# Setup of a cross-attention and expert kernel: TensorE multiplies by nought until the context is there, loads in order of need, query weights transposed between the keys' products

## The chip, the core and the metric

The kernel runs on one core of a Trainium2 chip. The metric is device time in microseconds (us). The engines of the core are TensorE (PE in the profile; PEld is its weight load), VectorE (DVE), ScalarE (ACT), GpSimd (POOL) and SyncE (SP), which here only issues transfers. Each engine works through its own instructions in order and waits on semaphores for the others; transfers (DMA) run in queues beside them. PSUM is the memory TensorE writes to, eight banks of which this kernel uses in turn; SBUF is the memory for everything else.

## The reference

Four sequences of 1024 tokens of width 256 attend to a context of 77 rows each, and then pass through a mixture of nine experts, two per token.

```
x = x + xattn(latents=layernorm(x), context=ctx)     # 16 heads of 64
    xn = layernorm(context) * ln1_w + ln1_b ;  ln = layernorm(latents) * ln2_w + ln2_b
    q = (ln @ Wq) * (1 + fside) + fside ;  k, v = split(xn @ Wkv)
    out = softmax(q k^T / 8) v @ Wout
x = x + moe(layernorm(x))                             # router, top 2 of 9, silu(x Wg) * (x Wu) @ Wd
```

All is float32. Since the context is short, the kernel folds Wq and the keys into one matrix per sequence (`g`, 256 by 16 x 77), and the values and Wout into another (`u`), so that a token needs only its normalised row times `g`, a softmax, and the weights times `u`. Building `g` and `u` is the setup; it is where the change lies.

## The kernel before, in words

The instructions of each engine stand in the order of the source (`tc.manual_schedule()`); the framework adds the semaphores. Four stages follow each other: the setup of `g` and then of `u` (to about 62 us), attention over 32 groups of 128 tokens with the routing of the group before mixed in, and the experts. TensorE passes from one to the next.

The setup up to `g`, with the lines of the profile:

- Constants. `make_identity` on GpSimd; on VectorE `eps_t`, 18 small memsets for `rank` and `base` (L109, L110), `ones`, `seen`.
- Loads. ScalarE issues `wrow` (ln2_w repeated on all partitions, L346) and `fs` (fside on all partitions, L350). SP issues the context `cx` in two transfers (L375), `wq_sb` in four, `wk_sb` in four (L380), then `wv_sb`, `wo_sb` and the first two groups of `x`. GpSimd issues ln1_w and ln1_b as columns `cw`, `cb` (L357), then `qb`, the router's weights, and a fill of a list in DRAM (L396).
- Context. Four BNStats and four aggregations on VectorE (L402, L404), a root on ScalarE (L408), and the normalised rows `cn`: sequences 0 and 2 on ScalarE (L444), 1 and 3 on VectorE (L439). TensorE transposes them into two banks `pct` (L452). ScalarE (L461) and VectorE (L456) each bring one of the two halves to SBUF as `cT`, times `cw` plus `cb`.
- Query weights. TensorE transposes `wq_sb` in 16 pieces into four banks `pwq` (L417), ahead of the context's transposes. VectorE multiplies them by `wrow` into `wqT` (L427): the first quarter before `cT`, the others between the keys' products. `wlast` (L498) is the last column negated, which ScalarE adds to each row (L503).
- Offsets. VectorE copies `fs` into `shift` by two copies (L471), makes `scale1` (L473) and scales `shift` (L474), and clears `cfold` (L476). In before they stand behind its half of `cT`. `scale1` is read by `kTs`.
- Keys. For each of eight pairs of heads TensorE makes `pk` from `wk_sb` and both halves of `cT` (L485), ScalarE copies it to `kT` (L489), VectorE scales it into `kTs` (L490).
- `g`. TensorE multiplies `wqT` by `kTs` (L626), and VectorE and ScalarE take the results out of PSUM in turn (L144, L146). In between stand the query offset `pcq`, the router's weights and a few tables.

A row of the trace such as `x32` for `pk` counts two records for each float32 matmul. On GpSimd, four memsets that the later stage needs follow the list's fill: `vbd`, `vrem` and two for `u` (L565 to L574). The first is held by hand until VectorE's last `cn` is done:

```
first = nc.gpsimd.memset(vbd, 0.0)
tc.add_manual_dep(first.ins, normed.ins.name, ...)
```

Of the kernel before, what the change touches and what calls it, by code (L numbers as in the profile page):

```python
# [8 lines left out]
F32 = mybir.dt.float32  # L9
I32 = mybir.dt.int32  # L10
U32 = mybir.dt.uint32
AF = mybir.ActivationFunctionType
ALU = mybir.AluOpType
AX = mybir.AxisListType

P = 128
# [5 lines left out]
def kernel(  # L22
# [18 lines left out]
    nc = tc.nc  # L41

    B, N, D = x.shape
    J = ctx_in.shape[1]
# [3 lines left out]
    E, _, FF = wg.shape  # L48
    C = D // P
    NP = H // 2  # L50
    TOK = B * N
    TB = 512
    NS = TB // P
# [41 lines left out]
    const = ctx.enter_context(tc.tile_pool(name="const", bufs=1))  # L95
# [5 lines left out]
    ident = const.tile([P, P], F32, name="ident")  # L101
    make_identity(nc, ident)
    eps_t = const.tile([P, 1], F32, name="eps_t")
    nc.vector.memset(eps_t, EPS)

    rank = const.tile([P, NS, E], F32, name="rank")
    base = const.tile([P, NS, E], F32, name="base")
    for e in range(E):
        nc.vector.memset(rank[:, :, e : e + 1], float(E - e))  # L109
        nc.vector.memset(base[:, :, e : e + 1], float(e * TOK))  # L110
    ones = const.tile([P, P], F32, name="ones")
    nc.vector.memset(ones, 1.0)
    seen = const.tile([P, E], F32, name="seen")
# [14 lines left out]
    def mm_tile(name):  # L128
        return ps_mm.tile([P, TB], F32, tag="mm", name=name)
# [3 lines left out]
    def bank_tile(name):  # L133

        turn_of[0] = (turn_of[0] + 1) % 8
        if turn_of[0] < 5:
            return mm_tile(name)
        k = turn_of[0] - 5
        return ps_sc.tile([P, TB], F32, tag=f"sc{k}", name=name)
# [10 lines left out]
    g_half, u_half = {}, {}  # L150
# [3 lines left out]
        u_half[i] = apool.tile([P, BH, KC, DE], F32, name=f"u{i}")  # L154
    g_sb = [g_half[b // BH][:, b % BH] for b in range(B)]
    u_sb = [u_half[b // BH][:, b % BH] for b in range(B)]

    def moments(src, n, name):
        k = src.shape[1]
        st = stat.tile([P, k, 6], F32, tag="bn", name=f"bn_{name}")  # L160
        mv = stat.tile([P, k, 2], F32, tag="mv", name=f"mv_{name}")
        for i in range(k):
            nc.vector.bn_stats(st[:n, i, :], src[:n, i, :])
        for i in range(k):
            nc.vector.bn_aggr(mv[:n, i, :], st[:n, i, :])
        return mv
# [175 lines left out]
    with tc.tile_pool(name="vside", bufs=1) as vside, ExitStack() as kvs:  # L342
        kside = kvs.enter_context(tc.tile_pool(name="kside", bufs=1))

        wrow = kside.tile([P, D], F32, name="wrow")
        nc.scalar.dma_start(  # L346
            out=wrow, in_=ln2_w.rearrange("(o d) -> o d", o=1).to_broadcast([P, D])
        )
        fs = vside.tile([P, B, NP, 2], F32, name="fs")
        nc.scalar.dma_start(  # L350
            out=fs.rearrange("p b n t -> p (b n t)"),
            in_=fside.rearrange("(o b) h -> o (b h)", o=1).to_broadcast([P, B * H]),
        )

        def column(eng, name, src):
            t = vside.tile([P, C], F32, name=name)
            eng.dma_start(out=t, in_=src.rearrange("(c p) -> p c", p=P))  # L357
            return t


        junk = const.tile([P, 1], F32, name="junk")
        nc.scalar.activation(junk, eps_t, AF.Sqrt)
        wq_sb = kside.tile([P, C, INNER], F32, name="wq_sb")
        wk_sb = kside.tile([P, C, INNER], F32, name="wk_sb")

# [5 lines left out]
        wq_v = wq.rearrange("(c p) n -> p c n", p=P)  # L371
        quarter = INNER // 4
        for i in range(2):
            at = slice(i * BH, (i + 1) * BH)
            nc.sync.dma_start(out=cx[:J, at], in_=ctx_in[at].rearrange("b j d -> j b d"))  # L375
        wk_v = wkv[:, :INNER].rearrange("(c p) n -> p c n", p=P)
        for dst, src in ((wq_sb, wq_v), (wk_sb, wk_v)):
            for k in range(4):
                at = slice(k * quarter, (k + 1) * quarter)
                nc.sync.dma_start(out=dst[:, :, at], in_=src[:, :, at])  # L380
        nc.sync.dma_start(out=wv_sb, in_=wkv[:, INNER:].rearrange("(c p) n -> p c n", p=P))
        nc.sync.dma_start(out=wo_sb[:, :, :D], in_=wout.rearrange("(n p) d -> p n d", p=P))

        cw, cb = column(nc.gpsimd, "cw", ln1_w), column(nc.gpsimd, "cb", ln1_b)

        qb = kside.tile([P, C, P // QT], F32, name="qb")
        nc.gpsimd.memset(qb, 0.0)
# [21 lines left out]

        wqT = kside.tile([P, NP, D], F32, name="wqT")  # L410
        cT = vside.tile([P, C, B * J], F32, name="cT")
        pwq = []
        for n in range(0, NP, 2):
            pt = bank_tile(f"pwq{n}")
            for k in range(2):
                for c in range(C):
                    nc.tensor.transpose(  # L417
                        pt[:, k * D + c * P : k * D + (c + 1) * P],
                        wq_sb[:, c, (n + k) * P : (n + k + 1) * P], ident,
                    )  # L420
            pwq.append(pt)

        def scale_queries(k):
            nc.vector.tensor_tensor(  # L427
                wqT[:, 2 * k : 2 * k + 2, :], pwq[k].rearrange("p (n d) -> p n d", n=2),
                wrow.unsqueeze(1).to_broadcast([P, 2, D]), ALU.mult,
            )  # L430

        nc.vector.reciprocal(cr[:J], csd[:J])
        nc.vector.scalar_tensor_tensor(
# [1 line left out]
        )  # L435
        cn = kside.tile([P, B, D], F32, name="cn")
        for b in range(B):
            if b % 2:
                normed = nc.vector.tensor_scalar(  # L439
                    cn[:J, b, :], cx[:J, b, :], cmv[:J, b, 0:1], cr[:J, b : b + 1],  # L440
                    ALU.subtract, ALU.mult,
                )
            else:
                nc.scalar.activation(  # L444
                    cn[:J, b, :], cx[:J, b, :], AF.Identity,
                    bias=cm[:J, b : b + 1], scale=cr[:J, b : b + 1],
                )
        scale_queries(0)
        for c in range(C):
            pt = bank_tile(f"pct{c}")  # L450
            for b in range(B):
                nc.tensor.transpose(  # L452
                    pt[:, b * J : (b + 1) * J], cn[:J, b, c * P : (c + 1) * P], ident[:J, :J]
                )
            if c:
                nc.vector.tensor_scalar(  # L456
                    cT[:, c, :], pt[:, : B * J], cw[:, c : c + 1], cb[:, c : c + 1],
                    ALU.mult, ALU.add,
                )
            else:  # L460
                nc.scalar.activation(  # L461
                    cT[:, c, :], pt[:, : B * J], AF.Identity,
                    bias=cb[:, c : c + 1], scale=cw[:, c : c + 1],
                )


        shift = kside.tile([P, NP, B], F32, name="shift")
        scale1 = kside.tile([P, NP, B], F32, name="scale1")
# [7 lines left out]
        nc.vector.memset(cfold_all, 0.0)  # L476
        cfold = cfold_all[:, :, : 2 * B].rearrange("p n (t b) -> p n t b", t=2)

        wlast = kside.tile([P, NP], F32, name="wlast")
        kT = kside.tile([P, NP, B * J], F32, name="kT")  # L480
        kTs = kside.tile([P, NP, B * J], F32, name="kTs")
        for n in range(NP):
            pk = bank_tile(f"pk{n}")
            for c in range(C):
                nc.tensor.matmul(  # L485
                    pk[:, : B * J], wk_sb[:, c, n * P : (n + 1) * P], cT[:, c, :],
                    start=(c == 0), stop=(c == C - 1),
                )
            nc.scalar.copy(kT[:, n, :], pk[:, : B * J])  # L489
            nc.vector.tensor_tensor(  # L490
                kTs[:, n, :].rearrange("p (b j) -> p b j", b=B),
                pk[:, : B * J].rearrange("p (b j) -> p b j", b=B),
                scale1[:, n, :].unsqueeze(2).to_broadcast([P, B, J]), ALU.mult,
            )
            if n < NP // 2 - 1:
                scale_queries(n + 1)
            elif n == NP // 2 - 1:
                nc.vector.tensor_scalar(  # L498
                    wlast, wqT[:, :, D - 1], -1.0, None, ALU.mult
                )  # L500
            if n >= NP // 2:
                for m in (2 * n - NP, 2 * n - NP + 1):
                    nc.scalar.activation(  # L503
                        wqT[:, m, :], wqT[:, m, :], AF.Identity, bias=wlast[:, m : m + 1]
                    )

        crow = kside.tile([P, D], F32, name="crow")
        cq = kside.tile([P, NP], F32, name="cq")
# [1 line left out]
        for c in range(C):  # L510
            for q in range(QT):
# [3 lines left out]
                    start=(c == 0), stop=(c == C - 1),  # L515
# [57 lines left out]
        for i in range(2):  # L573
# [4 lines left out]
            out=before, in_=ones, pattern=[[1, P]], compare_op=ALU.is_gt, fill=0.0, base=0,  # L578
# [36 lines left out]
        for n in range(NP):  # L615
# [6 lines left out]
            for c in range(C):  # L622
                for t in range(2):
# [4 lines left out]
                        start=True, stop=True,  # L628
                    )
                    h = 2 * n + t  # L630
                    src = pg[:, : B * J].rearrange("p (b j) -> p b j", b=B)
                    at = slice(h * J, (h + 1) * J)
# [14 lines left out]
        for b in range(B):  # L647
            nc.vector.tensor_copy(g_sb[b][:, :, HJ:], wz)
            for t in range(2):
                for k in range(NP // QT):  # L650
                    nc.sync.dma_start(
                        out=g_sb[b][P - 1 : P, C - 1, :HJ].rearrange(
                            "p (k q t j) -> p k q t j", q=QT, t=2, j=J
                        )[:, k, :, t, :],
                        in_=brow.rearrange("(q r) k m -> q r k m", q=QT)[
                            :, t * B + b, k, b * J : (b + 1) * J
                        ],
# [871 lines left out]
```

## Time and profile before

| | us |
|---|---|
| median of 3 runs | 926.22 (924.8 to 926.23) |
| profiled execution: its own time | 927.51 |
| profiled execution: span, first to last instruction | 925.8 |
| TensorE busy | 904.9 (98%) |
| VectorE busy | 450.6 (49%) |
| ScalarE busy | 341.3 (37%) |
| GpSimd busy | 319.6 (35%) |
| first TensorE instruction with work | 7.07 |
| first keys' product | 12.54 |
| first product for `g` | 23.66 |
| first eviction of `g` on VectorE | 24.52 |

The shares are of the whole span, and the setup before `g` is under 3% of it. A row of the timeline reads: start in us, duration in us, engine, line, operation, written tile <- read tiles, shape, number of instructions merged, and in brackets how long the engine sat idle before it and what ended that. An engine with a `q` at its end (SPq, ACTq) is its issuing of transfers.

### The profile page before, as it was taken

The numbers are of one execution on the slowest core, as the hardware profiler recorded it, in microseconds if no ns is written. First come the engines' busy times: TensorE is split into PE (matmuls) and PEld (weight loads), VectorE is DVE, ScalarE is ACT, GpSimd is POOL, SyncE is SP. The second block draws the span as 40 slices with busy tenths as digits, with TensorE's granted clock in tenths as the row PEclk, the third lists the DMA queues.
The fourth block names the chain that finished last, engine by engine and source line by source line (L and its number), as shares of the span: only waits on it lengthen the run. The fifth ranks groups of instructions, "written<-read, shape, count | busy, mean of one in ns | idle before, by whom it ended". The sixth has DMA issues, their size and how long they took to land. (4 is left out here: it accounts for less than half of the span.)

```text
span 925.8 us, 13336 instructions
## 1 busy us (share of the span) xinstructions
PE 904.9 (98%) x4190; PEld 702.2 (76%) x4190; DVE 450.6 (49%) x1325; ACT 341.3 (37%) x1076; POOL 319.6 (35%) x331
## 2 busy tenths in 40 slices
PE   6999999999999999999999999999999999999996
PEld 4676777777777777788888778778777778888885
DVE  5776677888788987753622222222222222222221
ACT  3667465665646565551211122222222211112210
POOL 6000000321504241146554434435435435444432
PEclk9999999999999999999999999999999999999998
DMA  8000010502112610456779779779779777779722
GB/s 262 24 2 1 2 68 24 46 24 46 47 23 69 225 32 24 117 146 175 182 197 309 210 210 305 212 211 311 223 204 305 221 209 221 221 219 311 223 38 23
DMA packets 110895, 137.05 MB, mean 148 GB/s; under 512 B 24483, under 2 KB 81321, under 8 KB 110826
## 3 DMA queue, kind: packets, MB, share of 16 engines
q1 hardware_dynamic: 93130, 118.78, 42.0%
q0 software_dynamic: 17408, 17.26, 10.3%
q8 instruction: 34, 0.56, 0.3%
q14 instruction: 35, 0.29, 0.1%
q10 hardware_dynamic: 288, 0.16, 0.1%
HBM read 119.51 MB, written 18.33 MB: 149 GB/s over the span
## 5 line engine op out<-in xcount | busy, mean ns | idle before, releaser
L1168 PE MATMUL pg<-xT,wgu 128*128 128x256 f32 x1144 | 251.8, 380 | 0.4 <-PEq L1485 0.4
L1168 PEld LDWEIGHTS pg<-xT,wgu 128*128 128x128 f32 x1144 | 216.3, 190 | 28.9 <-issue 0.8
L1242 PE MATMUL po<-wd,hid 128*128 128x256 f32 (+1 forms) x804 | 180.5, 380 | 0.0
L1242 PEld LDWEIGHTS po<-wd,hid 128*128 128x128 f32 (+1 forms) x804 | 147.4, 187 | 21.0 <-issue 0.7
L261 ACT ACTIVATE ex<-psc,mx 128x77 f32<-128x77 f32 x512 | 123.8, 361 | 102.0 <-DVE mx L251 96.8
L1277 POOL DMA_INDIRECT out_dram<-co,ids x63 | 100.7, 1598 | 169.1 <-DVE co L1245 135.7
L893 POOL DMA_INDIRECT list_d<-r_entry,r_pli x64 | 67.2, 1050 | 256.9 <-DVE r_pli L891 124.9
L324 PE MATMUL po<-u,aT 128*128 128x265 f32 x640 | 151.7, 391 | 1.0 <-ACT aT L313 0.8
L247 PE MATMUL psc<-g,zT 128*128 128x462 f32 (+1 forms) x384 | 139.1, 511 | 1.2 <-ACT zT L236 1.2
L324 PEld LDWEIGHTS po<-u,aT 128*128 128x128 f32 x640 | 118.9, 190 | 23.6 <-ACT aT L313 1.9
L1175 DVE TENSOR_TENSOR hid<-pg,sl 128x256 f32<-128x256 f32 x130 | 55.0, 424 | 160.2 <-ACT sl L1174 160.0
L1174 ACT ACTIVATE sl<-pg 128x256 f32<-128x256 f32 x130 | 49.7, 383 | 218.4 <-PE pg L1168 212.0
L247 PEld LDWEIGHTS psc<-g,zT 128*128 128x128 f32 x384 | 72.6, 190 | 59.1 <-issue 49.3
L1245 DVE TENSOR_SCALAR co<-po,ids 128x256 f32<-128x256 f32 x67 | 32.4, 484 | 137.5 <-PE po L1242 137.4
L1126 POOL DMA_INDIRECT yin<-y_d,ids x67 | 70.5, 1053 | 23.9 <-issue 16.4
L251 DVE TENSOR_REDUCE mx<-psc 128x6 f32<-128x462 f32 (+1 forms) x96 | 55.7, 581 | 18.3 <-PE psc L247 15.4
L281 DVE TENSOR_REDUCE sm<-ex 128x16 f32<-128x1232 f32 x32 | 45.9, 1435 | 36.6 <-ACT ex L261 36.1
L313 ACT COPY aT<-pa 128x512 f32<-128x512 f32 (+1 forms) x96 | 49.4, 552 | 27.2 <-PE pa L305 27.2
L305 PEld LDWEIGHTS pa<-ident,an 128*128 128x128 f32 x320 | 36.9, 141 | 7.7 <-PE po L324 1.4
L305 PE MATMUL pa<-ident,an 128*128 128x128 f32 x320 | 40.2, 273 | 1.0 <-DVE an L285 1.0
L285 DVE TENSOR_TENSOR an<-ex,rs 128x1024 f32<-128x1024 f32 x32 | 39.2, 1225 | 1.1
L1230 ACT COPY hid<-ph 128x384 f32<-128x384 f32 x15 | 7.2, 478 | 73.9 <-PE ph L1225 73.9
(306 smaller groups left out, 837.2 us busy)
## 6 DMA issues: line engine op xcount, KB each, us to landing
wgu<-in_L_ffn_Wg_dram SPq DMA_DIRECT2D x41, 704.0 KB
wd<-in_L_ffn_Wd_dram SPq DMA_DIRECT2D x41, 640.0 KB
wgu<-in_L_ffn_Wu_dram SPq DMA_DIRECT2D x41, 512.0 KB
wgu<-in_L_ffn_Wu_dram SPq DMA_DIRECT2D x41, 128.0 KB
x<-in_x_dram SPq DMA_DIRECT2D x8, 512.0 KB
out_dram<-x SPq DMA_DIRECT2D x8, 512.0 KB
y_d<-y SPq DMA_DIRECT2D x8, 512.0 KB
w<-in_L_ffn_Wg_dram SPq DMA_DIRECT2D x5, 704.0 KB
```

Source lines behind the costliest of these rows:

```text
L247: nc.tensor.matmul(psc[:, :w], zT[:, c, :], g_sb[i // NS // GPB][:, c, h * J : h * J + w], start=(c == 0), stop=(c == C - 1),)
L251: nc.vector.tensor_reduce(nmx[i][:, h : h + n], psc[:, : n * J].rearrange("p (h j) -> p h j", h=n), AX.X, ALU.max, negate=True,)
L261: nc.scalar.activation(exs[i][:, h + q, :], pscs[k][:, q * J : (q + 1) * J], AF.Exp, bias=nmx[i][:, h + q : h + q + 1],)
L305: nc.tensor.transpose(pa[:, q * P : (q + 1) * P], ans[i][:, (k + q) * P : (k + q + 1) * P], ident)
L324: nc.tensor.matmul(po[:, :DE], aT[:, n, :], u_sb[b][:, n, :], start=(n == 0), stop=(n == KC - 1))
L893: i = nc.gpsimd.indirect_dma_start(out=list_d[:, :], out_offset=bass.IndirectOffsetOnAxis(ap=place_i[:, s : s + 1], axis=0), in_=entries[k ...
L1126: return nc.gpsimd.indirect_dma_start(out=dst, out_offset=None, in_=src, in_offset=bass.IndirectOffsetOnAxis(ap=offsets, axis=0), **kw,)
L1168: nc.tensor.matmul(pg[:, g, :], w[:, c, at : at + P], xT[:, c, :], start=(c == 0), stop=(c == C - 1),)
L1174: nc.scalar.activation(sl, pg[:, 0, :], AF.Silu)
L1175: nc.vector.tensor_tensor(hid[:, f, :], pg[:, 1, :], sl, ALU.mult)
L1242: nc.tensor.matmul(po[rows, :D], hid[:, f, at], d[:, f, :], start=(f == 0), stop=(f == NF))
L1277: i = nc.gpsimd.indirect_dma_start(out=out_r, out_offset=bass.IndirectOffsetOnAxis(ap=rows_of(j, h, rows), axis=0), in_=cos[j][:, h, :], i ...
```

## The change

- TensorE gets eight products of a cleared piece of `u_half[0]` with itself (`warm`): five at once, three behind two small transposes. `rank` and `base` are set behind the memset that clears that piece.
- ln1_w and ln1_b come as two rows `crows` on ScalarE's queue, and TensorE transposes them into columns (`pc`, copied to `cwb` by VectorE), in place of the column transfers on GpSimd's queue.
- SP loads the keys' weights ahead of the query weights, each in two transfers instead of four. `wrow` is issued by ScalarE behind its `cn`; `fs` behind the table load.
- `cn`: one sequence on ScalarE and three on VectorE.
- `shift`, `scale1` and `cfold` stand ahead of the context's transposes in the source, so ahead of VectorE's half of `cT` in its order.
- The transposes of the query weights no longer stand first on TensorE: from the fifth keys' product on, one quarter follows each product, with its scaling and its part of `wlast` on VectorE and, one step later, its addition on ScalarE.
- What follows from the allocation: the first transfer of `x` now waits until the buffers of the setup are given back; in before it stood in SP's queue with no such wait.

```diff
-    rank = const.tile([P, NS, E], F32, name="rank")
...
+    WARM = 8
+    idle = u_half[0][:, 0, 0, :D]
+    nc.vector.memset(idle, 0.0)
+
+    def warm(ks):
+        for k in ks:
+            nc.tensor.matmul(
+                bank_tile(f"warm{k}")[:, :D], idle[:, :P], idle, start=True, stop=True
+            )
+
+    warm(range(2 * WARM // 3))
+
+    rank = const.tile([P, NS, E], F32, name="rank")
...
-        wrow = kside.tile([P, D], F32, name="wrow")
-        nc.scalar.dma_start(
-            out=wrow, in_=ln2_w.rearrange("(o d) -> o d", o=1).to_broadcast([P, D])
-        )
+        crows = kside.tile([2, D], F32, name="crows")
+        for k, src in enumerate((ln1_w, ln1_b)):
+            nc.scalar.dma_start(out=crows[k : k + 1, :], in_=src.rearrange("(o d) -> o d", o=1))
+
+        junk = const.tile([P, 1], F32, name="junk")
+        nc.scalar.activation(junk, eps_t, AF.Sqrt)
+
         fs = vside.tile([P, B, NP, 2], F32, name="fs")
         nc.scalar.dma_start(
...
-        for dst, src in ((wq_sb, wq_v), (wk_sb, wk_v)):
-            for k in range(4):
-                at = slice(k * quarter, (k + 1) * quarter)
+        for dst, src in ((wk_sb, wk_v), (wq_sb, wq_v)):
+            for k in range(2):
+                at = slice(2 * k * quarter, 2 * (k + 1) * quarter)
                 nc.sync.dma_start(out=dst[:, :, at], in_=src[:, :, at])
...
-        cw, cb = column(nc.gpsimd, "cw", ln1_w), column(nc.gpsimd, "cb", ln1_b)
...
-        pwq = []
-        for n in range(0, NP, 2):
-            pt = bank_tile(f"pwq{n}")
-            for k in range(2):
+        cwb = kside.tile([P, C, 2], F32, name="cwb")
+        pc = bank_tile("pc")
+        for c in range(C):
+            nc.tensor.transpose(
+                pc[:, 2 * c : 2 * c + 2], crows[:, c * P : (c + 1) * P], ident[:2, :2]
+            )
+
+        warm(range(2 * WARM // 3, WARM))
+
+        def turn_queries(k):
+            pt = bank_tile(f"pwq{k}")
+            for n in range(2):
                 for c in range(C):
                     nc.tensor.transpose(
...
+        def scale_queries(k, pt):
+            two = slice(2 * k, 2 * k + 2)
             nc.vector.tensor_tensor(
-                wqT[:, 2 * k : 2 * k + 2, :], pwq[k].rearrange("p (n d) -> p n d", n=2),
+                wqT[:, two, :], pt.rearrange("p (n d) -> p n d", n=2),
                 wrow.unsqueeze(1).to_broadcast([P, 2, D]), ALU.mult,
             )
+            nc.vector.tensor_scalar(wlast[:, two], wqT[:, two, D - 1], -1.0, None, ALU.mult)
+
+        def take_last(k):
+            for n in (2 * k, 2 * k + 1):
+                nc.scalar.activation(
+                    wqT[:, n, :], wqT[:, n, :], AF.Identity, bias=wlast[:, n : n + 1]
+                )
...
-            if b % 2:
+            if b:
                 normed = nc.vector.tensor_scalar(
...
-        scale_queries(0)
+        nc.vector.tensor_copy(cwb.rearrange("p c k -> p (c k)"), pc[:, : 2 * C])
+        nc.scalar.dma_start(
+            out=wrow, in_=ln2_w.rearrange("(o d) -> o d", o=1).to_broadcast([P, D])
+        )
+
+        shift = kside.tile([P, NP, B], F32, name="shift")
+        scale1 = kside.tile([P, NP, B], F32, name="scale1")
+        for t in range(2):
+            half = slice(64 * t, 64 * t + 64)
+            nc.vector.tensor_copy(shift[half], fs[half, :, :, t].rearrange("p b n -> p n b"))
+
+        nc.vector.tensor_scalar(scale1, shift, ATT_SCALE, ATT_SCALE, ALU.mult, ALU.add)
+        nc.vector.tensor_scalar(shift, shift, ATT_SCALE, None, ALU.mult)
+        cfold_all = kside.tile([P, NP, P // QT], F32, name="cfold")
+        nc.vector.memset(cfold_all, 0.0)
...
         for c in range(C):
             pt = bank_tile(f"pct{c}")
...
-        shift = kside.tile([P, NP, B], F32, name="shift")
...
-            if n < NP // 2 - 1:
-                scale_queries(n + 1)
-            elif n == NP // 2 - 1:
-                nc.vector.tensor_scalar(
-                    wlast, wqT[:, :, D - 1], -1.0, None, ALU.mult
-                )
-            if n >= NP // 2:
-                for m in (2 * n - NP, 2 * n - NP + 1):
-                    nc.scalar.activation(
-                        wqT[:, m, :], wqT[:, m, :], AF.Identity, bias=wlast[:, m : m + 1]
-                    )
+            k = n - TURN
+            if k >= 0:
+                scale_queries(k, turn_queries(k))
+            if k >= 1:
+                take_last(k - 1)
+        take_last(NP - 1 - TURN)
```

More of the change, by code (lines that the diff above doesn't have):

```diff
@@ L104 @@
     nc.vector.memset(eps_t, EPS)
-    rank = const.tile([P, NS, E], F32, name="rank")
[L107 to L110, printed above, removed]
     ones = const.tile([P, P], F32, name="ones")
@@ L156 @@
     u_sb = [u_half[b // BH][:, b % BH] for b in range(B)]
+    WARM = 8
[8 more added lines that the diff above has]
+    rank = const.tile([P, NS, E], F32, name="rank")
+    base = const.tile([P, NS, E], F32, name="base")
+    for e in range(E):
+        nc.vector.memset(rank[:, :, e : e + 1], float(E - e))
+        nc.vector.memset(base[:, :, e : e + 1], float(e * TOK))
     def moments(src, n, name):
@@ L353 @@
         )
[L355 to L362, printed above, removed]
+        wrow = kside.tile([P, D], F32, name="wrow")
         wq_sb = kside.tile([P, C, INNER], F32, name="wq_sb")
@@ L411 @@
         cT = vside.tile([P, C, B * J], F32, name="cT")
-        pwq = []
-        for n in range(0, NP, 2):
-            pt = bank_tile(f"pwq{n}")
-            for k in range(2):
+        cwb = kside.tile([P, C, 2], F32, name="cwb")
[8 more added lines that the diff above has]
+            for n in range(2):
                 for c in range(C):
                     nc.tensor.transpose(
-                        pt[:, k * D + c * P : k * D + (c + 1) * P],
-                        wq_sb[:, c, (n + k) * P : (n + k + 1) * P], ident,
-                    )
-            pwq.append(pt)
-        def scale_queries(k):
+                        pt[:, n * D + c * P : n * D + (c + 1) * P],
+                        wq_sb[:, c, (2 * k + n) * P : (2 * k + n + 1) * P], ident,
+                    )
+            return pt
+        wlast = kside.tile([P, NP], F32, name="wlast")
+        def scale_queries(k, pt):
+            two = slice(2 * k, 2 * k + 2)
             nc.vector.tensor_tensor(
-                wqT[:, 2 * k : 2 * k + 2, :], pwq[k].rearrange("p (n d) -> p n d", n=2),
+                wqT[:, two, :], pt.rearrange("p (n d) -> p n d", n=2),
                 wrow.unsqueeze(1).to_broadcast([P, 2, D]), ALU.mult,
             )
+            nc.vector.tensor_scalar(wlast[:, two], wqT[:, two, D - 1], -1.0, None, ALU.mult)
[4 more added lines that the diff above has]
+                )
         nc.vector.reciprocal(cr[:J], csd[:J])
@@ L447 @@
                 )
-        scale_queries(0)
[L449 to L453, printed above, removed]
-                )
[L455 to L458, printed above, removed]
-                )
[L460 to L464, printed above, removed]
+        nc.vector.tensor_copy(cwb.rearrange("p c k -> p (c k)"), pc[:, : 2 * C])
+        nc.scalar.dma_start(
+            out=wrow, in_=ln2_w.rearrange("(o d) -> o d", o=1).to_broadcast([P, D])
+        )
         shift = kside.tile([P, NP, B], F32, name="shift")
@@ L477 @@
         cfold = cfold_all[:, :, : 2 * B].rearrange("p n (t b) -> p n t b", t=2)
-        wlast = kside.tile([P, NP], F32, name="wlast")
+        for c in range(C):
+            pt = bank_tile(f"pct{c}")
+            for b in range(B):
+                nc.tensor.transpose(
+                    pt[:, b * J : (b + 1) * J], cn[:J, b, c * P : (c + 1) * P], ident[:J, :J]
+                )
+            if c:
+                nc.vector.tensor_scalar(
+                    cT[:, c, :], pt[:, : B * J], cwb[:, c, 0:1], cwb[:, c, 1:2],
+                    ALU.mult, ALU.add,
+                )
+            else:
+                nc.scalar.activation(
+                    cT[:, c, :], pt[:, : B * J], AF.Identity,
+                    bias=cwb[:, c, 1:2], scale=cwb[:, c, 0:1],
+                )
+        TURN = NP - NP // 2
         kT = kside.tile([P, NP, B * J], F32, name="kT")
@@ L494 @@
             )
-            if n < NP // 2 - 1:
-                scale_queries(n + 1)
-            elif n == NP // 2 - 1:
-                nc.vector.tensor_scalar(
-                    wlast, wqT[:, :, D - 1], -1.0, None, ALU.mult
-                )
-            if n >= NP // 2:
-                for m in (2 * n - NP, 2 * n - NP + 1):
-                    nc.scalar.activation(
-                        wqT[:, m, :], wqT[:, m, :], AF.Identity, bias=wlast[:, m : m + 1]
-                    )
+            k = n - TURN
[4 more added lines that the diff above has]
+        take_last(NP - 1 - TURN)
         crow = kside.tile([P, D], F32, name="crow")
```

## The prediction

> **What bounds the kernel now.** I read the chain of work that ended last first, then the timeline of the first 35 us by engine, because every changed line lies there.
>
> ```profile
> PE 3%; issue 2%; DMA 1%; POOL 1%; POOLq 0%
> ...
> PE   6999999999999999999999999999999999999996
> ```
>
> The chain does not follow the start, but TensorE's row of the slice view does: only the first slice (23 us) is below 9 tenths. From there to the end TensorE is the line everything hangs on, so a microsecond gained or lost in the setup should reach the end whole. The setup itself, from the timeline (start, duration, engine, line):
>
> ```profile
> 7.10 4.22 PE L417 MATMUL pwq<-ident,wq_sb 128*128 128x128 f32 x16 [7.10 <-DMA wq_sb<-in_L_xattn_Wq_dram]
> 11.12 1.24 PE L452 MATMUL pct<-ident,cn 77*128 77x77 f32 x8
> 12.54 10.19 PE L485 MATMUL pk<-cT,wk_sb 128*128 128x308 f32 x32 [0.18 <-ACT cT L461]
> ...
> 14.24 0.34 PEld L485 LDWEIGHTS pk<-cT,wk_sb 128*128 128x128 f32 x1 [0.18 <-issue]
> 14.76 0.34 PEld L485 LDWEIGHTS pk<-cT,wk_sb 128*128 128x128 f32 x1 [0.17 <-issue]
> ...
> 15.78 6.46 PEld L485 LDWEIGHTS pk<-cT,wk_sb 128*128 128x128 f32 x25 [0.18 <-issue]
> ```
>
> Two costs: the context's transposes (pct) stand behind the query weights' transposes, whose last load lands at 10.2 us; and of the 32 records of the keys' products the first 7 come 0.515 us apart, the other 25 6.46/25 = 0.258 apart. TensorE ran at half speed until 15.78: 7 x 0.257 = 1.8 us lost.
>
> The third view is VectorE beside GpSimd, and it decides my forecast:
>
> ```profile
> 8.69 3.51 POOL L565 MEMSET vbd<- 128x4096 f32 x1 [1.45 <-DVE cn L439]
> 12.13 0.95 POOL L572 MEMSET vrem<- 128x1024 f32 x1
> 13.03 1.01 POOL L574 MEMSET u<- 128x1060 f32 x1
> 13.99 1.01 POOL L574 MEMSET u<- 128x1060 f32 x1
> ...
> 12.40 0.60 DVE L456 TENSOR_SCALAR cT<-pct,cw,cb 128x308 f32<-128x308 f32 x1 [3.17 <-PE pct L452]
> 12.91 1.16 DVE L471 COPY shift<-fs 64x32 f32<-64x32 f32 x2
> 13.13 0.95 DVE L471 COPY shift<-fs 64x32 f32<-64x32 f32 x1
> 14.11 0.93 DVE L473 TENSOR_SCALAR scale<-shift 128x32 f32<-128x32 f32 x1
> 15.07 0.22 DVE L474 TENSOR_SCALAR shift<-shift 128x32 f32<-128x32 f32 x1
> ```
>
> A copy of 32 elements takes 0.95 us and a scaling of 32 takes 0.93, where the same scaling one line later takes 0.22. The two long ones end at 14.08 and 15.04; GpSimd's memsets end at 14.04 and 15.00. Each ran until 0.04 us after the memset that had begun before it.
>
> [...] cT from PSUM ran inside vrem's memset without waiting. [...] The trace shows the rise (15.78)[...].
>
> **The change part by part.**
>
> *Loads.* GpSimd loses the issues of cw and cb (0.94 + 0.78 us), ScalarE gains two issues of one row each for crows (0.39 each, as wrow) and loses wrow for now. fs moves behind the table load: issued near 3.3 instead of 1.25. GpSimd's list fill ends 1.7 us sooner. SP issues 4 fewer transfers, keys' weights first; the first 512 KB, which took to about 8.3 as query weights, are needed at 10.1. Hidden, all of it. wrow out of the way (128 KB) may bring cx in earlier, 0 to 0.6 us by the 215 GB/s of that stretch; I take 0.2.
>
> *rank and base* (18 memsets, 0.03 apart, 0.5 us) go behind one 256-wide memset (0.27). VectorE is free until 5.37: nothing.
>
> *Warming.* Eight products of 256 columns: at half clock 2 x 0.515 x 256/308 = 0.86 us each, at most 6.8 us, from 1.5 to 8.3 at the latest. TensorE idled until 7.07 and is next needed near 8.8: nothing. pc adds two tiny transposes inside.
>
> *cn.* VectorE takes three of four (+0.32 at its spacing 7.90 to 8.22). Its last ends at E = 8.62 + 0.32 - 0.2 = 8.75. pct at full clock ends about E + 0.35, ScalarE's half of cT at E + 1.15, and the first keys' product starts near 10.1. wrow's issue on ScalarE (0.39) fits in between. This is 2.4 us before 12.54.
>
> *The offsets, moved ahead of VectorE's half of cT.* Every keys' product needs both halves. VectorE's order is now cn, cwb, shift, shift, scale1, shift, cfold, cT. GpSimd's vbd memset still waits for the last cn and so starts 0.07 after it (8.62 to 8.69 in before), at 8.82, to 12.33. cwb is a small PSUM copy begun 0.07 before E; the first shift copy follows some 0.09 later, just ahead of the memset; the second some 0.09 after that, just behind it. Then: second copy until 12.36; scale1 behind vrem (0.88 later) until 13.24; the last shift behind the first u memset until 14.20; cfold and the step to the next instruction 0.20; cT 0.60, to 15.0; its product at 15.2. If both copies get in first, all is 0.95 earlier; if none does (or fs lands after 8.75), 0.95 later. So cT is ready 2.0 us later than before's 13.0 (1.1 to 3.0), and the gain above is gone. What queues behind it is all of TensorE.
>
> *Query transposes.* 16, at 0.107 us each at full clock (the woT transposes' weight loads: 0.86 us for 8), now between keys' products: +1.71 on the path, where they hid behind loads. VectorE's scaling (0.68) and wlast (0.16) follow each, 1.3 us a step with kTs against TensorE's 1.03 + 0.43: hidden except after the last.
>
> *Sum at full clock.* 15.2 + 30 records x 0.258 = 7.74, + 1.71, gives 24.65. The last keys' product ends at 24.2; kT, kTs, the last scaling (0.20 + 0.41 + 0.50 + 0.62), wlast and a memset put VectorE's first eviction of g at 26.25, against 24.52. From there VectorE is busy back to back to 34.1 in before, so it sets the pace: +1.7 us. ScalarE, 2 us late with crow, has 8.1 us of evictions in that stretch to VectorE's 9.6 and catches up.
>
> *The clock.* TensorE now idles from about 10.6 to 15.2, after little work since 8. Unknown cost: 0 if the clock holds, 1.8 as in before if it falls [...]. I take 1.8[...]. Total +3.5.
>
> *Later.* The first x load must now wait until the setup's buffers are given back (GpSimd's first memset in that place starts at 34.85), instead of 8.93; it is read at 44.41. Even at cx's 4.5 us from issue to landing it is there near 40. The 16 short row transfers on SP behind it slip by two issues (0.44 each) from an end at 43.5; first needed in the scores after 60. Nothing, with 4 us to spare.
>
> **Rivals.** (1) [...] the offsets take 0.6 us, cT is there at 10.5, keys' products run from 10.1 at full clock: 10.1 + 8.25 + 1.71 = 20.1, VectorE's first eviction 21.65, -2.9 us: 923.4, faster. It decides where cT's second half ends before about 13.3 at full clock. Against it: two rows five times their length, ending with memsets. For it: only that the first copy is short. (2) *Late cT, clock kept*: the same stall without the 1.8: +0.8 to +2.7, 927.0 to 928.9, or no measurable change if both copies get in. [...] (3) *The warming does nothing lasting [...]*: -2.9 + 1.8 = -1.1, 925.1, no change. A late x load would cost its excess over 4 us; I see none.
>
> **How the numbers follow.** The sums stand against the profiled execution (span 925.8, its own time 927.5); the median of the runs is 926.22, and since all is a shift in the start I add to that: 926.2 + 3.5 = 929.7. Late cT with the clock fallen: 0.52 (both copies in +2.6, one +3.5, none +4.5[...]); late cT, clock kept: 0.34; rival 1: 0.09; rival 3: 0.05. About 0.2% (1.85 us) is what a measurement of this kernel can tell from no change. Clock kept splits: 0.17 below that bound, 0.17 above. So faster 0.10, same 0.22, slower 0.68. The range leaves out rival 1 below [...]: 925.5 to 931.5.
>
> **What would show it.** After: scale1 and a shift copy each about 0.9 us or longer, ending with memsets, one of them near 3.5; cT's second half ending 14 to 16; TensorE without work from about 10.6; products 0.515 apart after it if the clock fell; first pct and first keys' product before 10.5. I am wrong if the offsets take 0.2 us each between 8.8 and 9.8, if GpSimd's vbd memset starts later than they, or if something after 35 us waits for x.

## The result, and the profile after

The median went from 926.23 us (10 runs, 924.8 to 927.65) to 929.16 us (10 runs, 928.04 to 930.5): 2.9 us more, ratio 1.0029 with a 95% interval of 1.0019 to 1.0038. The kernel is slower by a little, clear of the noise. Here and below a ratio with its interval is not the quotient of the two medians beside it, and can differ from it by up to 0.0006. The profiled executions, 927.51 before and 929.22 after, have spans of 925.8 and 927.2.

The difference arises in the first 28 us. VectorE's first eviction of `g` begins at 27.24 instead of 24.52, +2.72 (timeline of after, VectorE):

```profile
27.24 1.92 DVE L138 COPY g<-pgk 128x154 f32<-128x154 f32 x7 [0.40 <-PE pgk L651]
```

The first scores that TensorE makes in the attention loop begin 2.81 later (timelines of before and of after, TensorE):

```profile
64.56 1.82 PE L247 MATMUL psc<-g,zT 128*128 128x462 f32 x4 [0.72 <-ACT zT L236]
```

```profile
67.37 1.82 PE L261 MATMUL psc<-g,zT 128*128 128x462 f32 x4 [0.72 <-ACT zT L250]
```

TensorE's first product of the experts is still 2.77 later (398.69 against 395.92). From there on the two profiles differ by waits far from the setup: at 715.47, for example, the profile of before waits 0.47 for a load (`yin`) for which the profile of after does not wait, and the last products lie only 1.54 apart. From its first to its last product the experts' stage took 521.5 us in the profile of before and 520.3 in that of after. That is why one execution against another says little about 1 us, and why the setup is read from the traces below and the worth of a change from many runs.

The slice view of the kernel after has TensorE a little busier in the first slice (it multiplies noughts there) and the same 9s behind it:

```profile
PE   7999999999999999999999999999999999999996
```

So the setup is where to look. The timeline of after, VectorE and GpSimd (start, duration, engine, line, written <- read):

```profile
6.94 3.51 POOL L590 MEMSET vbd<- 128x4096 f32 x1 [1.38 <-DVE cn L466]
9.10 2.31 DVE L484 COPY shift<-fs 64x32 f32<-64x32 f32 x2 [2.15 <-DMA fs<-in_fside_Bx_dram]
10.39 0.99 POOL L597 MEMSET vrem<- 128x1024 f32 x1
11.32 1.97 POOL L599 MEMSET u<- 128x1060 f32 x2
11.44 0.93 DVE L486 TENSOR_SCALAR scale<-shift 128x32 f32<-128x32 f32 x1
12.41 0.92 DVE L487 TENSOR_SCALAR shift<-shift 128x32 f32<-128x32 f32 x1
12.77 0.56 DVE L499 TENSOR_SCALAR cT<-pct,cwb 128x308 f32<-128x308 f32 x1
13.06 0.27 DVE L489 MEMSET cfold<- 128x256 f32 x1
```

All four small operations on `fs` and `shift` now take 0.91 to 1.38 us, and each ends with a memset: `scale1` at 12.37 (first `u` memset: about 12.33), the last `shift` at 13.33 (second: 13.29). VectorE's half of `cT` ends with it, at 13.33; the other half had been done by ScalarE at 7.91. TensorE in the same timeline:

```profile
6.83 0.70 PE L495 MATMUL pct<-ident,cn 77*128 77x77 f32 x8
10.11 0.76 PE L515 MATMUL pk<-cT,wk_sb 128*128 128x308 f32 x2 [2.58 <-DMA wk_sb<-in_L_xattn_Wkv_dram]
13.41 7.17 PE L515 MATMUL pk<-cT,wk_sb 128*128 128x308 f32 x18 [2.54 <-DVE cfold L489]
...
17.17 0.34 PEld L515 LDWEIGHTS pk<-cT,wk_sb 128*128 128x128 f32 x1 [0.18 <-issue]
17.68 2.42 PEld L515 LDWEIGHTS pk<-cT,wk_sb 128*128 128x128 f32 x9 [0.18 <-issue]
```

The context is transposed by 7.5, against 12.4 before. Half a product can be made at 10.11; the other half waits for `cT` until 13.41. From then nine records take 4.27 us, to 17.68, where at full clock, 0.258 a record, they would take 2.32. The stage view of after shows why, one row a microsecond; the number behind the five engines is the granted clock:

```profile
core 0: us, PE busy (x) PEld busy (x) DVE busy (x) ACT busy (x) POOL busy (x), PEclk, DMA share, GB/s
10.00:11.00 1.00, 0.76 (x2) 0.30 (x2) 0.99 (x2) 0.00 (x0) 1.00 (x2) 1.00 1.06 408
11.00:12.00 1.00, 0.00 (x0) 0.00 (x0) 0.96 (x2) 0.00 (x0) 1.00 (x2) 0.57 1.06 404
12.00:13.00 1.00, 0.00 (x0) 0.00 (x0) 0.97 (x3) 0.00 (x0) 1.00 (x2) 0.50 1.04 411
...
17.00:18.00 1.00, 1.00 (x3) 0.66 (x2) 0.48 (x1) 0.31 (x1) 0.00 (x0) 0.51 0.70 240
18.00:19.00 1.00, 1.00 (x5) 0.72 (x5) 0.00 (x1) 0.42 (x1) 0.00 (x0) 1.00 0.38 129
```

The column reads 1.00 up to the first change that the profile recorded, so for the first microseconds the spacing of the records has to be taken instead: the weight loads of `warm` come 0.43 us apart until 4.19 and 0.21 to 0.22 apart from 4.48 on. The clock thus rose during the warming, was still full at 10.1 (two weight loads in 0.30, in 0.50 at 13.41), fell at about 11.15 (0.57 as the mean of that row) and stood at half until about 18, 6.8 us in all. TensorE's two idle stretches before and around the fall were 2.6 us (7.5 to 10.1) and 2.5 us (10.9 to 13.4), with the half product between them.

### The profile page after: what moved, and what is told of

The parts are those of the page before. It is cut to its first block, busy times and chain, and to the rows that moved or that the text cites. A ratio compares the mean times of both kernels' runs of the same rounds, so it can differ in the third digit from the quotient of the medians.

```text
span 927.2 us, 13369 instructions
## 1 busy us (share of the span) xinstructions
PE 907.9 (98%) x4208; PEld 704.1 (76%) x4208; DVE 453.3 (49%) x1331; ACT 341.6 (37%) x1075; POOL 318.9 (34%) x329
## 3 DMA queue, kind: packets, MB, share of 16 engines
q0 software_dynamic: 17344, 17.26, 10.4%
## 4 chain that ended last, share of the span: by engine, by line
PE 87%; DMA 5%; issue 3%; DVE 2%; ACT 1%; POOL 1%; SPq 0%; POOLq 0%; ACTq 0%
PE pg L1193 21%; PE po L1267 16%; PE po L338 15%; PE psc L261 14%; PE pa L319 3%; PE psg L1229 3%; PE psu L1229 3%; PE psb L1229 2%; DMA out_dram<-co,ids 2%; PE px L1179 2%; PE pu L739 1%; PE pk L515 1%; PE ph L1250 1%; DMA wd_r<-in_L_ffn_Wd_dram 1%; PE pgk L651 1%
```

## The experiments

Theory: GpSimd's memsets block the small offset operations (0.91 to 1.38 us each in the kernel after, ending with memsets; by what they block, no run shows), which makes `cT` late; in the wait the clock falls. Rivals: the order and the late `fs` alone make it late; or the query transposes between the products are the cost.

**Memsets held longer.** One dependency moves from the last `cn` to VectorE's half of `cT`:

```diff
-            first.ins, normed.ins.name,
+            first.ins, context.ins.name,      # context: VectorE's cT instruction
```

> GpSimd's memset of vbd (and with it the three behind it) is held until VectorE's half of cT is done instead of until its last cn; nothing else differs from the kernel after. Theory [...]: the copies start when fs lands (9.1) and take about 0.2 each, cT's second half ends near 10.5, keys' products run from 10.1 to 10.7 on at full clock, the first product for g moves from 26.4 to about 21, the time falls by 5 to 924 (2 below the kernel before). Rival one (the late fs and the order alone make cT late, the memsets do not): cT's second half still ends after 12.5 and the time stays within 1 of 929.2. Rival two (the query transposes between the products are the cost, the stall is not): the stall goes and the time falls by less than 1.5.

Measured: 923.81 us beside 925.88 for the kernel before, ratio 0.9978 (0.9971 to 0.9985). Its timeline:

```profile
8.63 0.37 DVE L484 COPY shift<-fs 64x32 f32<-64x32 f32 x2 [1.69 <-DMA fs<-in_fside_Bx_dram]
9.04 0.18 DVE L486 TENSOR_SCALAR scale<-shift 128x32 f32<-128x32 f32 x1
9.25 0.18 DVE L487 TENSOR_SCALAR shift<-shift 128x32 f32<-128x32 f32 x1
9.43 0.27 DVE L489 MEMSET cfold<- 128x256 f32 x1
9.62 0.42 DVE L499 TENSOR_SCALAR cT<-pct,cwb 128x308 f32<-128x308 f32 x1
...
9.70 5.42 PE L515 MATMUL pk<-cT,wk_sb 128*128 128x308 f32 x20 [1.57 <-DMA wk_sb<-in_L_xattn_Wkv_dram]
```

The same four operations take 0.18 us each. Twenty records of the products go through at full clock (5.42 us, where 19 x 0.258 and the last one's 0.42 make 5.32). The first eviction of `g` comes at 21.78, 5.5 earlier than in the kernel after. Nothing but the memsets' place differs, so the memsets are the cause of the loss; the first rival falls, and so does the second: the query transposes are still there. The late `fs` does keep `cT` until 10.04 here, but that costs next to nothing, because the first weights land only at 9.70.

**Offsets behind `cT` again**, memsets left where they were:

```diff
-        shift = ... scale1 = ... cfold = ...      # ahead of the context's transposes
         for c in range(C): ...                    # pct, cT
+        shift = ... scale1 = ... cfold = ...
```

> The offsets (shift, scale1, cfold) stand behind VectorE's half of cT again, as before; GpSimd's memsets are where they were. Theory: cT's second half ends near 8.2, the keys' products start when their weights land (10.1) at full clock; the offsets still run late behind the memsets (scale1 near 12.4), but only kTs waits for them, and TensorE has banks ahead: first product for g near 21, time 924. Rival one (the late fs makes the delay wherever the offsets stand): kTs is late instead and stops TensorE, 927 or more. Rival two (the query transposes): falls by less than 1.5.

Measured: 923.72, ratio 0.9976 (0.9963 to 0.9989). The timeline of this kernel:

```profile
8.27 0.60 DVE L487 TENSOR_SCALAR cT<-pct,cwb 128x308 f32<-128x308 f32 x1 [1.09 <-PE pct L483]
9.09 2.55 DVE L501 COPY shift<-fs 64x32 f32<-64x32 f32 x2 [0.23 <-DMA fs<-in_fside_Bx_dram]
11.67 0.93 DVE L503 TENSOR_SCALAR scale<-shift 128x32 f32<-128x32 f32 x1
12.64 0.92 DVE L504 TENSOR_SCALAR shift<-shift 128x32 f32<-128x32 f32 x1
...
10.11 5.42 PE L515 MATMUL pk<-cT,wk_sb 128*128 128x308 f32 x20 [1.89 <-DMA wk_sb<-in_L_xattn_Wkv_dram]
```

The offsets are held as long as ever, to 13.6, and it costs nothing: `cT`, inside `vbd` (7.17 to 10.68), is out of the way at 8.87, and only `kTs` waits (its first begins at 13.0), while 20 records of the products take 5.42 as with the memsets held. What matters here is not that VectorE is blocked but what stands behind the blocked instruction in its order.

**The gap bridged.** Thirteen more products of noughts between the context's transposes and the first `pk`:

```diff
+        for k in range(8):
+            pt = bank_tile(f"bridge{k}")
+            for _ in range(2 if k < 5 else 1):
+                nc.tensor.matmul(pt[:, :D], idle[:, :P], idle, start=True, stop=True)
```

> Thirteen more products of noughts (256 columns) stand between the context's transposes and the keys' first product; they fill the gap from 7.5 to about 13. The stall itself stays. Theory (two costs, the stall and the clock that falls in it): the keys' products after it come 0.26 apart from the first instead of 0.515 for nine records, the time falls by about 2.4 to 926.8. Rival (the clock is not kept by such products, or the lost clock costs nothing because VectorE sets the pace): 929 or above.

Measured: 928.0, ratio 1.0024 (1.0014 to 1.0034); first eviction at 26.05, 1.2 earlier than after, not 2.4. Its TensorE row:

```profile
14.04 5.35 PE L520 MATMUL pk<-cT,wk_sb 128*128 128x308 f32 x20
```

The products do run at full clock from the first (20 records in 5.35, with the memsets held 5.42). But the bridge ended late: the first product's weight load stands at 13.83, 0.4 later than in the kernel after, and the half product of 10.11 (0.5) was pushed behind the gap. With these the clock's part comes to 1.2 + 0.4 + 0.5 = 2.1, by the trace. The times of the two kernels alone do not separate: their intervals overlap.

**No products of noughts**, in the kernel after and in the one with the memsets held:

```diff
-    warm(range(2 * WARM // 3))
-        warm(range(2 * WARM // 3, WARM))
```

(The memset of the cleared piece goes with them.)

> No products of noughts at all; everything else as after. Theory: in the kernel after the warming is lost in the stall, so that leaving it out costs only pct at half clock (1.24 instead of 0.70), which the stall hides: within 0.5 of 929.2. Rival (the warming is worth its 2 us even so): 931 or more.

> The kernel e1_hold (memsets held until cT is done) without the products of noughts. Theory: without the stall the warming has its worth: the keys' products run at half clock at first, seven to nine records 0.26 longer each, 1.8 to 2.4, so 925.6 to 926.2, or about the kernel before. Rival (the warming is worth nothing since the gap between the context's transposes and the keys' products lets the clock fall again): within 0.5 of e1_hold's 923.8.

Measured: 929.05, ratio 1.0037 (1.0027 to 1.0047) in the first, first eviction at 26.90 against 27.24: in the kernel after, no worth of the warming can be seen. In the second 927.46 beside 927.89, ratio 0.9991 (0.9975 to 1.0007) against 0.9978 with it; the intervals overlap. By the traces the first eviction is at 23.98 against 21.78, and the first nine records of the products take 4.27, as slow as in the kernel after. So in this pair of traces the warming is worth 2.2 once the stall is gone. The times do not prove it, and a second profile of the held memsets, below, lost the clock in spite of the warming.

**`fs` first** on ScalarE's queue, to see the race between copy and memset with the input there:

```diff
+        fs = ... ; nc.scalar.dma_start(out=fs..., in_=fside...)
         crows = kside.tile([2, D], F32, name="crows")
```

> As after, but fs is issued first on ScalarE's queue, ahead of the two rows of crows, so that it should land before VectorE's last cn (6.9). Theory, as the prediction had it: the first shift copy then begins just ahead of GpSimd's vbd memset and is short (0.2), the second waits for vbd (to 10.5), scale1 for vrem (11.4), the last shift for the first u memset (12.4): all one memset earlier than after, cT ready near 12.5 instead of 13.3, time lower by 0.8 to 1 (928.2). If both copies get in ahead: cT near 11.5, 927.3. Rival (the copy loses against the memset even when its input is there): cT at 13.3, 929.2. If fs lands late all the same, the run says nothing on this.

Measured: 931.68 beside 927.89, ratio 1.0035 (1.0025 to 1.0045). The time did not fall, because `cx` landed at 5.30 instead of 3.50 and took everything with it. The race itself went as expected (timeline, then the answer for the tile, whose three figures are the shortest, median and longest duration in ns):

```profile
8.72 3.66 DVE L484 COPY shift<-fs 64x32 f32<-64x32 f32 x2
8.79 3.55 POOL L590 MEMSET vbd<- 128x4096 f32 x1 [3.22 <-DVE cn L466]
```

```profile
L484 DVE COPY shift<-fs x2: 170/1822/3474, 8.7 to 8.9; 64x32 f32<-64x32 f32 x2
```

The copy that began 0.07 ahead of the memset took 0.17; the one behind it took 3.47, to the memset's end.

**What let `cx` in early?** The kernel before with `wrow` issued late:

```diff
-        nc.scalar.dma_start(out=wrow, ...)        # first on ScalarE's queue
+        nc.scalar.dma_start(out=wrow, ...)        # behind the context's root
```

> The kernel before with one move: wrow (128 KB) is issued by ScalarE behind the context's root instead of first. It is to tell why cx landed at 3.5 instead of 5.4. Theory one (wrow's 128 KB stood in its way): cx is read by VectorE at 3.5 to 4.0. Theory two (the two loads of columns of four-byte pieces, which the change took away, did): still at 5.2 to 5.4. Since VectorE needs wrow ahead of its half of cT in this kernel, the time itself may rise by up to 3.

Measured: `cx` read at 5.31 (one run, 932.18 us; VectorE waited for `wrow` ahead of `cT`). So taking `wrow` away is not enough. The run with `fs` first has no column loads and no early `wrow`, differs from the kernel after only in the order of that queue, and reads `cx` at 5.30: an early `fs` is enough to make `cx` late. Whether the column loads or `wrow` would do the same beside a late `fs` was not tried. Over all profiles, with `fs` issued at 0.83 to 1.25 (four) `cx` was read at 4.84 to 5.37, and with `fs` issued at 1.69 or 1.70 (nine) at 3.41 to 3.73. The price is `fs` itself, which is then read between 8.1 and 9.4.

**Towards a better kernel.** First the held memsets with `fs` first and the weights in quarters:

```diff
-            for k in range(2):
-                at = slice(2 * k * quarter, 2 * (k + 1) * quarter)
+            for k in range(4):
+                at = slice(k * quarter, (k + 1) * quarter)
```

> e1_hold, and fs issued first, and the keys' and query weights loaded in quarters again. In e1_hold the keys' first product waited for fs (by cT) and for the first 512 KB of its weights, both near 9 to 10. Theory: with fs early cT is ready near 8.2 and the first 256 KB have landed by then, so the keys' products start near 8.3 instead of 9.7 and, fed a quarter at a time, lose little later: 1 to 1.5 below e1_hold, 922.5. Rival (the weights as a whole are the bound, so an earlier start only turns into later waits): 923.8.

Measured: 925.07 beside 927.89, ratio 0.9966 (0.9956 to 0.9975); first eviction at 21.79, the same as in the first experiment. The gain expected inside the setup was not there: early `fs` made `cx` late (4.84), and the products began at 9.68, against 9.70 there. The forecast of 1 to 1.5 less is not borne out.

Then offsets behind `cT`, memsets held until the last offset, weights in quarters, `fs` left late; and beside it, on the same chip, the first experiment and the kernel after again.

> The change with three things altered: the offsets behind VectorE's half of cT, GpSimd's memsets held until the last of the offsets [...], and both weights in quarters; fs stays where the change put it, behind the rows and the table load. Theory: cT ready at 8.1, the first quarter of the keys' weights there by then or a little later, so the keys' products start at 8.2 to 9 at full clock, kTs follow the offsets (fs near 9, scale1 near 9.6); first eviction of g on VectorE near 20.3 to 21 instead of 21.8 in e1_hold, time 0.8 to 1.5 below e1_hold beside it. Rival (the weights' arrival is the bound): equal to e1_hold within 0.4.

> e1_hold again, on the chip of e9_all: ratio to the kernel before 0.9978 as it was, within 0.0007.

> The kernel after again, on the chip of e9_all, so that the two above can be set against it: ratio to the kernel before 1.0029, within 0.0009; fs lands between 8 and 9.2 and VectorE's half of cT ends within 0.1 of the end of GpSimd's last long memset.

Measured beside 928.26 for the kernel before: 924.42, ratio 0.9956 (0.9944 to 0.9968); the held memsets 924.99, 0.9962 (0.9947 to 0.9978); the kernel after 929.94, 1.0023 (1.0013 to 1.0032). The first is the lowest ratio of the study, 0.4% below the kernel before and, by 924.42 against 929.94, 0.6% below the kernel after; from the held memsets alone it cannot be told apart, so the forecast of 0.8 to 1.5 us below them is not shown. Its timeline:

```profile
7.68 0.60 DVE L487 TENSOR_SCALAR cT<-pct,cwb 128x308 f32<-128x308 f32 x1 [0.63 <-PE pct L483]
8.20 0.36 DVE L501 COPY shift<-fs 64x32 f32<-64x32 f32 x2
...
9.10 5.42 PE L515 MATMUL pk<-cT,wk_sb 128*128 128x308 f32 x20 [1.45 <-DMA wk_sb<-in_L_xattn_Wkv_dram]
...
21.18 2.15 DVE L138 COPY g<-pgk 128x154 f32<-128x154 f32 x8 [0.40 <-PE pgk L651]
```

The keys' weights are what the products wait for now, 1.45 us, even in quarters.

The kernel after, taken again, missed its expectation in two points: `fs` was read at 9.27 instead of between 8 and 9.2, and `cT` did not end with the last long memset (13.41). Its timeline:

```profile
9.27 3.22 DVE L484 COPY shift<-fs 64x32 f32<-64x32 f32 x2 [2.16 <-DMA fs<-in_fside_Bx_dram]
...
13.48 0.22 DVE L487 TENSOR_SCALAR shift<-shift 128x32 f32<-128x32 f32 x1
13.69 0.27 DVE L489 MEMSET cfold<- 128x256 f32 x1
13.89 0.41 DVE L499 TENSOR_SCALAR cT<-pct,cwb 128x308 f32<-128x308 f32 x1
```

The first copy took 2.26 us: it was not let in at the change from `vbd` to `vrem` (10.60), as it was in the first profile (there at 10.45), but only at the end of `vrem` (11.49). `cT` ended at 14.30, 0.97 later. A slot of one memset can thus fall out either way in two executions of the same kernel. The held memsets, taken again, show the clock doing the same; the stage view of that run, the slowest of its eight (928.27, median 924.99):

```profile
10.00:11.00 1.00, 0.59 (x2) 0.42 (x3) 0.79 (x4) 0.00 (x0) 0.11 (x1) 1.00 1.05 398
11.00:12.00 1.00, 1.00 (x4) 0.76 (x4) 0.00 (x0) 0.03 (x1) 1.00 (x1) 0.66 1.07 410
12.00:13.00 1.00, 1.00 (x3) 0.64 (x3) 0.48 (x1) 0.39 (x1) 1.00 (x1) 0.50 1.06 419
...
14.00:15.00 1.00, 1.00 (x3) 0.64 (x3) 0.48 (x1) 0.42 (x1) 1.00 (x2) 0.64 1.05 382
15.00:16.00 1.00, 1.00 (x5) 0.76 (x4) 0.06 (x1) 0.42 (x1) 1.00 (x2) 1.00 1.07 378
```

After a gap of 2.8 us (7.6 to 10.4) the products began at full clock (weight loads 0.28 apart from 10.88, 0.51 from 11.73), lost it at about 11.3, in the middle of their work (0.66 as the mean of that row, then 0.50), and had it back near 14.7 (0.64, then 1.00), 3.4 later. In the first profile of the same kernel the gap was 1.6 (8.1 to 9.7) and the clock stayed (5.42 us for the first twenty records); first evictions 24.18 and 21.78. Of these 2.4, 0.7 is the later start of the products and 1.7 their first twenty records (7.11 instead of 5.42). The half-clock stretch was 3.4 here and 6.8 in the kernel after; no run shows what sets its length or its start.

## Why the prediction was right, point by point

The mechanism was the one foretold; that the sum came out close is in part luck. The central case (one copy ahead of the memset) did not happen. The case that did, no copy ahead, had been put 0.95 later, `cT` near 15.95 and +4.5 in all; an earlier context (-1.9) and no tail behind the last `shift` (-0.8) brought `cT` to 13.33.

- **Late `cT` behind the memsets**: right, and shown by moving the memsets alone. The terms were off: *cx earlier by 0.2*: it was 1.9 (3.50 instead of 5.37), so the last `cn` ended at 6.88, not 8.75. *fs in time for the copies*: it landed at 9.10; the case set out for that, none of the copies ahead of `vbd`, is what happened. It was issued at 1.69, not 3.3: the issue did not wait for the table load in front of it, which ran from 1.62 to 2.90. It then took 7.4 us. *cfold and cT, 0.8 us behind the last shift*: nothing; both ended with it. `cT` was ready at 13.33, not 15.0.
- **One copy ahead of the memset, one behind**: not reached in the kernel after; seen with `fs` first, 0.17 and 3.47 us, as worked out.
- **The clock falls, 1.8 us**: it fell; nine records lost 4.27 - 2.32 = 1.95 in the kernel after. By the bridge 2.1. That it would fall was the author's estimate, for one gap of 4.6 (10.6 to 15.2). `cT` came earlier than foretold, so the gaps were 2.6 and 2.5, with half a product between them; how long a gap brings the fall was not shown. And the 1.8 was misread from the profile of before: its first seven records take 12.54 to 15.78, 3.24 us, where 7 x 0.258 is 1.81, so that 1.4 was lost there, the first two having come in 0.68 together.
- **Query transposes, 1.71 on the path**: the four steps of product and transposes stand 1.48 apart (20.16, 21.64, 23.11, 24.59), the product takes 1.03, so 0.44 each, 1.78 in all.
- **Sum**: first eviction +2.72 for +3.5 predicted, time +2.9. A microsecond of the setup reached the experts whole (2.77 at 395.92); to the end it can be followed only in the medians.
- **Keys' weights landed by 8.3**: wrong. TensorE waited for them until 10.11; that the first product stood where it was foretold (10.1) is luck, since it had been put down to `cT`. The late weights cost nothing in the kernel after, where `cT` was later still, but they set the start of the products in four of the five profiles of repaired kernels with the warming (9.10 to 10.41).
- **Loads of x**: hidden, as said. Its reader on VectorE begins at 47.22, 2.81 after before's 44.41, the same shift as everything else.
- **Rival 1**, the offsets done in 0.6 us, was put at -2.9; taking the memsets away gives -2.1 in the median (923.81 - 925.88) and -2.7 at the first eviction. That is about what the other parts of the change are worth once this one step does not undo them. (The second profile of that kernel, with the clock fallen, has -0.3 at the first eviction.)

## What to carry to other kernels

When a tiny VectorE operation lasts as long as a GpSimd one beside it and ends just after it, as here (0.93 us instead of 0.18, ending 0.04 after a memset), suspect that it is blocked. Count not its own length but that of the GpSimd instruction it can meet (3.47 us behind `vbd`), possibly of the next one too (2.26 us over the rest of `vbd` and `vrem`), and look at what stands behind it in VectorE's order. Moved "into idle time" ahead of a critical eviction, such work put that eviction behind GpSimd too (`cT` at 13.33, with the memsets held at 10.04); either hold the filler memsets until the critical step is done, or keep the operations that are blocked behind it. As for the warming, in the traces it was worth 2.2 us (first evictions 21.78 and 23.98) where the products began 1.6 after the context's transposes. In the kernel after, with idle stretches of 2.6 and 2.5, leaving it out made no difference (1.0037 against 1.0029, intervals overlapping).

## What the runs showed that was not expected

- Behind a blocked `shift`, the eviction of `cT` from PSUM and the memset of `cfold` are recorded as begun while it was still blocked, and all three end at 13.33; TensorE went on at 13.41. The two did not have to be done one after the other after the release. With `fs` first the same: `shift` and `cT` both end at 14.26. Where the last `shift` was not blocked, in the second profile of the kernel after, `cT` ended 0.60 after it (13.70 and 14.30).
- A transfer of 32 KB (`fs`, 128 rows of 256 bytes, all from the same source) went with the context by its place in the queue: `cx` is read at 3.4 to 3.7 where `fs` is issued late and at 4.8 to 5.4 where it is issued early. Why it costs so much is open.
- The clock of TensorE is not settled by the kernel alone: in the kernel with the memsets held, TensorE kept full clock in one execution and lost 1.7 us by a fall in another.
